# A cross-attention and mixture-of-experts kernel: two experts take 256 tokens each before the routing is complete

## The chip, the cores and the metric

The kernel runs on one core of a Trainium2 chip, in 32-bit floating point. A time is the device time of one execution in microseconds; where a median is given, it is over three executions. The profile is of one more execution, recorded with every instruction and every DMA.

The engines are TensorE (PE, with its weight loads as PEld), VectorE (DVE), ScalarE (ACT), GpSimd (POOL) and SyncE (SP, which here only issues DMAs and loads registers). Each takes its own instructions in the order of the built program, and waits on semaphores for the others. SP, ACT and POOL issue DMAs into queues of their own.

## What is computed

`x` is 8 batches of 256 tokens, 512 wide. Attention over a second input comes first (32 heads of 16, 8 groups), then 32 experts of which each token takes four. Every pair of experts shares a smaller one.

```python
x = x + xattn(layernorm(x), ctx, ctx)            # Wq, Wk, Wv, softmax, Wfc, bfc
h = layernorm(x)
logits = h @ gate_w.T                            # 32 experts
w, sel = top4(softmax(logits)); w = w / w.sum()
large = sum over e of w_e * (silu(h @ Wg[e]) * (h @ Wu[e])) @ Wd[e]            # 192 wide
small = sum over e of w_e * (silu(h @ cWg[e//2]) * (h @ cWu[e//2])) @ cWd[e//2]  # 128 wide
out = x + large + 0.05 * small
```

There are 2048 x 4 = 8192 pairs of token and expert. How many each expert gets depends on the data.

## The kernel before

**Stage 1, attention.** One loop runs over the slots: 16 for each batch, in which the score products of one part, the softmax of the part ten slots earlier (`LAG`) and one or two other steps of other batches (`slots`, L553) are issued in an order that is written out by hand. The wrappers `pe`, `dve` and `act` (class `InOrder`, L39) keep that order for TensorE, VectorE and ScalarE. The steps of a tile of 128 tokens after its attention are those of `finish`: `turn` (transpose), `fc0` and `fc1` (output projection, then the normalised `row`, which goes to the DRAM tensor `xn_all`), `turn_h`, `route` (L472: logits, the best four, their weights) and `place` (L511: for each of its four choices a place in that expert's list, and on POOL one indirect DMA for each choice that scatters token number and weight into the DRAM tensor `lists`, L536). `lists` has room for 2048 entries for each expert; its first 512 entries were filled with numbers of empty rows (`NO_ONE`), which stand behind the tokens in `xn_all` and `out`.

The loop routes the tiles up to number 13. The last two, 14 and 15, are finished behind the loop (L647 to 655), one step after another, with `dve` and `act` no longer held to the written order.

**Ranking, L659 to 682.** TensorE sums `taken` (the choices of all tokens) to `count`; a few VectorE operations compare all counts with one another to `rank` and `at_rank`; one more product gives `order`, the experts by size.

**Stage 2, the experts.** The experts run one after another (L961). The program is built with fixed shares: `CAPS` (L28) lists how many pairs the largest, the second largest and so on may have; `RANKS` puts the two smallest first. For the n-th expert SP loads its number into a register (`expert`), then fetches its list (`list_of`, L707) and its weights (`weights_of`, L694: `wm` 1280 KB and `sm` 768 KB, in four buffers). POOL gathers its rows, one indirect DMA for each 128 (`tokens_of`, L717, line 720). TensorE transposes them (`turned`, `ept` at L744), and does five products of 128 columns of weights by the share's tokens (`inner`, L754: `pu_g`, `pu_u`, `pu_ug`, `pu_gs`, `pu_us`, L764). `down` (L796) does the second products `py`: for two full tiles together at L851, 854 and 856, for a remainder of up to 64 at L839 to 843. `evict` (L804) scales them by the pair's weight and stores them with an indirect DMA on POOL that adds to `out` (L820). The stores of one expert wait for those of the expert before (L977 to 985), since they may add to the same rows. The transposes of the next expert lie between the products of this one.

An expert with more pairs than its share leaves tiles over: `beyond` (L861) works out which, and a loop at the end (L991) handles them, one tile of 128 at a time, as many times as a register says.

SP's issues at the start of stage 2 come in the order that the code has them, from L954 on:

```python
for i in range(3):
    fetch_list(i)
fetch_weights(0)
fetch_tokens(0)
fetch_weights(1)
fetch_tokens(1)
fetch_weights(2)
fetch_list(3)
```

Of the kernel before, what the change touches and what calls it, by code (L numbers as in the profile page):

```python
# [10 lines left out]
F32 = mybir.dt.float32  # L11
I32 = mybir.dt.int32
U32 = mybir.dt.uint32
AF = mybir.ActivationFunctionType
ALU = mybir.AluOpType
# [10 lines left out]


CAPS = [400, 352, 336] + [320] * 3 + [304] * 4 + [288] * 4 + [272] * 5  # L28
CAPS += [256] * 2 + [240] * 6 + [224] * 3 + [208, 192]

# [32 lines left out]
def xattn_moe(ctx: ExitStack, tc, x, ctxT, wqT, wkT, wvT, wfcT, bfc, gateT, wx, ws, out):  # L63
# [35 lines left out]
    def counting(name, n, step, per_partition, base=0):  # L99
# [7 lines left out]
    token_i, _ = counting("token", NT, P, 1)  # L107
# [13 lines left out]
    nc.vector.memset(nothing, 0.0)  # L121

# [3 lines left out]
        no_one[:, :, 0].bitcast(I32), [[1, NO_ONE]], base=B * S, channel_multiplier=0  # L126
# [15 lines left out]
    with ExitStack() as att:  # L142
        aw = att.enter_context(tc.tile_pool(name="aw", bufs=1))
        a2 = att.enter_context(tc.tile_pool(name="a2", bufs=2))
        a3 = att.enter_context(tc.tile_pool(name="a3", bufs=3))
        a6 = att.enter_context(tc.tile_pool(name="a6", bufs=6))
# [43 lines left out]
        def load_ctx(b):  # L190
            t = a3.tile([P, KC, S], F32, tag="ctx", name=f"ctx_{b}")
            nc.scalar.dma_start(out=t, in_=kmajor(ctxT)[:, :, b * S : (b + 1) * S])
            return t

        wq_sb = aw.tile([P, KC, E], F32, tag="wq", name="wq_sb")
        wk_sb = aw.tile([P, KC, P], F32, tag="wk", name="wk_sb")
        wv_sb = aw.tile([P, KC, P], F32, tag="wv", name="wv_sb")
# [22 lines left out]
        def norm(t):  # L220

            xns[t] = a2.tile([P, E], F32, tag=f"xn{t % 2}", name=f"xn_{t}")
            of = statistics(acc[t], f"a{t}")

            def scale():
                scaled(xns[t], acc[t], of)
                nc.gpsimd.tensor_tensor(acc[t], acc[t], bfc_sb, ALU.add)

            later.append(scale)

        def project(b):
# [6 lines left out]
            xT = a2.tile([P, KC, S], F32, tag="xT", name=f"xT_{b}")  # L238
            qT = [a3.tile([P, KC, S], F32, tag=f"qT{r}", name=f"qT_{b}_{r}") for r in range(2)]
            kT = a2.tile([P, 2, S], F32, tag="kT", name=f"kT_{b}")  # L240
            k1 = a3.tile([P, 2, S], F32, tag="k1", name=f"k1_{b}")
# [179 lines left out]
        def finish(t):  # L421
# [12 lines left out]
            def fc(h):  # L434
                half = slice(h * (E // 2), (h + 1) * (E // 2))
                pm = ps_m.tile([P, E // 2], F32, tag="pm", name=f"pmf_{t}_{h}")
                for kc in range(KC):
                    pe.matmul(
                        pm,
                        lhsT=box["oT"][:, kc, :],  # L440
                        rhs=wfc_sb[:, kc, half],
                        start=(kc == 0),
                        stop=(kc == KC - 1),
                    )
                dve.tensor_tensor(acc[t][:, half], pm, acc[t][:, half], ALU.add)
                if h == 0:
                    return
                row = box["row"] = a3.tile([P, E], F32, tag="row", name=f"row_{t}")

                def stats():  # L450
                    of = statistics(acc[t], f"f{t}")
                    act.dma_start(out=out[t * P : (t + 1) * P, :], in_=acc[t])

                    def scale():
                        scaled(row, acc[t], of)
                        later.append(
                            lambda: act.dma_start(out=xn_all[t * P : (t + 1) * P, :], in_=row)
                        )

                    later.append(scale)  # L460

                later.append(stats)
# [84 lines left out]


# [37 lines left out]

        slots_of = {s: what for s, what in enumerate(first)}
# [33 lines left out]
        for s in range(16 * B + LAG + 6):  # L621
# [12 lines left out]
            if s == len(first):  # L634
# [5 lines left out]
                    out=xn_all[B * S :, :].rearrange("(j p) r -> p j r", p=P),  # L640
                    in_=nothing.unsqueeze(1).to_broadcast([P, NS, E]),
                ))
            if slot == 4 and b + 2 < B:
                load_x(b + 2)
                ctxs[b + 2] = load_ctx(b + 2)

        dve, act = nc.vector, nc.scalar  # L647
        last = [finish(t) for t in (NT - 2, NT - 1)]
        for i, name in (
            (0, "turn"), (1, "turn"), (0, "fc0"), (0, "fc1"), (1, "fc0"), (1, "fc1"),  # L650
            (0, "turn_h"), (0, "route"), (1, "turn_h"), (0, "place"), (1, "route"), (1, "place"),
        ):
            last[i][name]()
            while later:
                put_off()

        pm = ps_m.tile([NE, 1], F32, tag="pm", name="pm_count")  # L659
        pe.matmul(pm, lhsT=taken, rhs=ones[:, :1], start=True, stop=True)  # L660
        pr = ps_m.tile([NE, NE], F32, tag="pm", name="pm_counts")
        pe.matmul(pr, lhsT=ones[:, :NE], rhs=taken, start=True, stop=True)
        count = const.tile([NE, 1], F32, tag="count", name="count")
        nc.vector.tensor_copy(count, pm)
        key = const.tile([NE, 1], F32, tag="key", name="key")
        nc.vector.scalar_tensor_tensor(
            key, count, float(NE), part_f[:NE], ALU.mult, ALU.subtract
        )
        more = const.tile([NE, NE], F32, tag="more", name="more")
        nc.vector.scalar_tensor_tensor(  # L670
            more, pr, float(NE), iota_e[:NE], ALU.mult, ALU.subtract
        )
        nc.vector.tensor_scalar(more, more, key, None, ALU.is_gt)
        rank = const.tile([NE, 1], F32, tag="rank", name="rank")
        nc.vector.tensor_reduce(rank, more, AX.X, ALU.add)
        at_rank = const.tile([NE, NE], F32, tag="at_rank", name="at_rank")
        nc.vector.tensor_scalar(at_rank, iota_e[:NE], rank, None, ALU.is_equal)

        pm = ps_m.tile([1, NE], F32, tag="pm", name="pm_order")
        pe.matmul(pm, lhsT=part_f[:NE], rhs=at_rank, start=True, stop=True)  # L680
        order = const.tile([1, NE], I32, tag="order", name="order")
        nc.vector.tensor_copy(order, pm)


    wts = ctx.enter_context(tc.tile_pool(name="wts", bufs=4))
    m1 = ctx.enter_context(tc.tile_pool(name="m1", bufs=1))
    m2 = ctx.enter_context(tc.tile_pool(name="m2", bufs=2))
    m3 = ctx.enter_context(tc.tile_pool(name="m3", bufs=3))
    m6 = ctx.enter_context(tc.tile_pool(name="m6", bufs=6))
    ps_x = ctx.enter_context(tc.tile_pool(name="ps_x", bufs=2, space=bass.MemoryType.PSUM))  # L690
    ps_u = ctx.enter_context(tc.tile_pool(name="ps_u", bufs=3, space=bass.MemoryType.PSUM))
    ps_y = ctx.enter_context(tc.tile_pool(name="ps_y", bufs=3, space=bass.MemoryType.PSUM))

    def weights_of(e_r, n, after=None):  # L694
# [9 lines left out]
        nc.sync.dma_start(out=sm, in_=ws[bass.ds(e_r, 1), :, :].rearrange("o p n -> (o p) n"))  # L704
# [32 lines left out]
    def turned(n, rows, ns):  # L737
# [3 lines left out]
        def chunk(kc):  # L741
            pt = ps_x.tile([P, NS * P], F32, tag="pt", name=f"ept_{n}_{kc}")
            for j in range(ns):
                nc.tensor.transpose(  # L744
# [9 lines left out]
    def inner(n, xT, wm, sm, acts, w, between=lambda kc: None):  # L754
# [6 lines left out]
        def product(cols, name):  # L761
            pu = ps_u.tile([P, NS * P], F32, tag="pu", name=f"pu_{n}_{name}")
            for kc in range(KC):
                nc.tensor.matmul(  # L764
# [96 lines left out]
    def beyond():  # L861
# [8 lines left out]
        nc.vector.tensor_copy(has[:, 1:2], count)  # L870
        nc.vector.tensor_reduce(has[:, 2:3], ps, AX.X, ALU.add)
        over = m1.tile([NE, 1], F32, tag="over", name="over")
        nc.vector.tensor_tensor(over, count, has[:, 2:3], ALU.subtract)
# [32 lines left out]
        done = m1.tile([P, 1], F32, tag="done", name="done")  # L906
        nc.vector.tensor_tensor(done, lo[:, 0:1], lo[:, 1:2], ALU.subtract)
# [6 lines left out]
        nc.sync.dma_start(out=tbl_f, in_=done)  # L914
# [8 lines left out]
    def expert(i):  # L923
        if ("expert", i) not in held:
# [3 lines left out]
        return held["expert", i]  # L928

    def fetch_list(i):  # L930
        if i < NE:
            entries = lists.rearrange("(e n) c -> e n c", e=NE)[
                bass.ds(expert(i), 1), : ns_of[i] * P, :
            ]
            held["list", i] = list_of(
                entries.rearrange("o n c -> (o n) c"), i, ns_of[i],
# [3 lines left out]
    def fetch_weights(i):  # L940
        if i < NE:
            held["weights", i] = weights_of(expert(i), i, gathers.get(i - 1) if i < 3 else None)
# [4 lines left out]


    for i in range(3):
        fetch_list(i)  # L950
    fetch_weights(0)
    fetch_tokens(0)
    fetch_weights(1)
    fetch_tokens(1)  # L954
    fetch_weights(2)
    fetch_list(3)
    now = turned(0, held["tokens", 0], ns_of[0])
    for kc in range(KC):
        now[1](kc)
    before = []  # L960
    for i in range(NE):  # L961
        fetch_tokens(i + 2)
        fetch_weights(i + 3)
        fetch_list(i + 4)
        wm, sm = held["weights", i]
        acts = units[i % 2]
        if i + 1 < NE:
            then = turned(i + 1, held["tokens", i + 1], ns_of[i + 1])
            inner(i, now[0], wm, sm, acts, SHARES[i], then[1])
        else:  # L970
            inner(i, now[0], wm, sm, acts, SHARES[i])
        now = then
        li = held["list", i]
        stores = down(i, acts, wm, sm, li, lambda j: li[:, j, 1:2], SHARES[i])
# [11 lines left out]
        before = stores  # L986
# [88 lines left out]
```

## Time and profile before

| | us |
|---|---|
| median of three executions (lowest, highest) | 1044.01 (1042.89, 1044.69) |
| the profiled execution | 1044.12 |
| its span, first to last instruction | 1042.2 |

| engine | busy us of the span | instructions |
|---|---|---|
| PE | 973.0 (93%) | 4960 |
| PEld | 583.9 (56%) | 4960 |
| DVE | 410.4 (39%) | 918 |
| POOL | 320.7 (31%) | 333 |
| ACT | 317.1 (30%) | 553 |

The mean granted TensorE clock is 0.975 of full. DMA moves 129.39 MB in all.

How to read what follows. The page has rows of 40 digits: the span in 40 slices of 26 us, each digit the busy share in tenths (9 is 90% or more); in the row PEclk it is the clock that TensorE was granted, in tenths of full speed. A line of the timeline gives start, length, engine and line of the code, the operation with its output and input, the count, and in brackets how long the engine was idle before it and what ended that. In the chain of waits, which is followed back from the last instruction, each piece is start, length and what it was. PE instructions are counted as two records for a 32-bit product: a product over four blocks of 128 rows shows as x8. Stage 1 ends at about 462 us of the span, and the first product of stage 2 starts at 504.9.

### The profile page before, as it was taken

Reading aid. Unit: us, or ns where it says so; the run is one execution under the profiler, and the core shown is the slowest. Engines: PE = TensorE matmul, PEld = TensorE weight load, DVE = VectorE, ACT = ScalarE, POOL = GpSimd, SP = SyncE. Lnnn points to the kernel's source line nnn. Section 1 sums busy time; section 2 is a strip of 40 time slices with the busy share of each in tenths; the row PEclk is TensorE's granted clock in tenths of the full one; section 3 lists DMA queues with packets and bytes.
Section 4 is the critical chain, followed back from the end, with each engine's and each line's share of the span. In section 5 each row is a group of like instructions: output and inputs, shape, how many; then the busy total and the mean of one; then the engine's idle time right before and its main releaser. Section 6 shows DMA issues by size and latency. Waiting matters only on the chain.

```text
span 1042.2 us, 13463 instructions
## 1 busy us (share of the span) xinstructions
PE 973.0 (93%) x4960; PEld 583.9 (56%) x4960; DVE 410.4 (39%) x918; ACT 317.1 (30%) x553; POOL 320.7 (31%) x333
## 2 busy tenths in 40 slices
PE   6989999999999997993799999999999999999994
PEld 4534555555555653452565565656666666777772
DVE  4555666666676657433122122212222222122220
ACT  2245544545454544440211121111121212111110
POOL 4100131313121203033352524444343434433221
PEclk9999999999999999996799999999999999999998
DMA  6301010101010000001986775767676767777622
GB/s 214 107 2 42 31 52 32 52 32 33 31 32 21 23 12 32 11 32 43 401 294 134 212 201 168 227 172 207 181 218 187 212 176 209 232 220 224 183 37 36
DMA packets 56197, 129.39 MB, mean 124 GB/s; under 512 B 20545, under 2 KB 25922, under 8 KB 52034
## 3 DMA queue, kind: packets, MB, share of 16 engines
q1 hardware_dynamic: 26802, 75.21, 20.1%
q0 software_dynamic: 18912, 40.12, 18.3%
q10 hardware_dynamic: 10416, 13.18, 3.5%
q8 instruction: 40, 0.66, 0.3%
q14 instruction: 27, 0.22, 0.1%
HBM read 100.56 MB, written 27.66 MB: 123 GB/s over the span
## 4 chain that ended last, share of the span: by engine, by line
PE 50%; issue 1%; DMA 1%; POOL 1%; DVE 0%; POOLq 0%; ACT 0%
PE pu_g L764 6%; PE py L856 6%; PE pu_us L764 6%; PE pu_gs L764 6%; PE pu_ug L764 6%; PE pu_u L764 6%; PE py L851 5%; PE ept L744 4%; PE py L854 3%; PE py L839 2%; PE py L843 1%; DMA rows<-xn_all,li 1%; POOL lists L536 0%; POOL out_dram L820 0%; DVE exT L750 0%
## 5 line engine op out<-in xcount | busy, mean ns | idle before, releaser
L49 DVE TENSOR_REDUCE mx<-sc 128x4 f32<-128x1024 f32 x128 | 156.6, 1223 | 92.9 <-PE st L49 69.9
L49 ACT ACTIVATE pT<-st 128x1024 f32<-128x1024 f32 x128 | 131.0, 1024 | 143.5 <-PE st L49 137.3
L49 PE MATMUL sc<-kT,qT 32*128 32x512 f32 x512 | 145.4, 644 | 17.4 <-DVE mx L49 16.2
L820 POOL DMA_INDIRECT out_dram<-y,li x84 | 128.5, 1529 | 93.3 <-ACT y L818 75.0
L720 POOL DMA_INDIRECT rows<-xn_all,li x84 | 82.3, 980 | 237.2 <-DMA li<-lists 98.3
L49 PE MATMUL st<-qT,k 32*128 32x512 f32 x512 | 146.4, 648 | 0.5 <-DMA qT<-mT 0.5
L536 POOL DMA_INDIRECT lists<-ent,slot_i x64 | 62.4, 975 | 107.8 <-DVE slot_i L49 87.4
L750 DVE COPY exT<-ept 128x384 f32<-128x384 f32 (+2 forms) x64 | 32.5, 508 | 115.6 <-PE ept L744 114.7
L818 ACT ACTIVATE y<-py,li 128x512 f32<-128x512 f32 (+2 forms) x35 | 24.0, 687 | 174.4 <-PE py L856 161.8
L744 PE MATMUL ept<-ident,rows 128*128 128x128 f32 x336 | 59.0, 279 | 19.1 <-DMA rows<-xn_all,li 18.7
L816 DVE TENSOR_SCALAR y<-py,li 128x512 f32<-128x512 f32 (+3 forms) x31 | 23.3, 750 | 129.5 <-PE py L856 129.5
L49 PEld LDWEIGHTS sc<-kT,qT 32*128 32x128 f32 x512 | 38.5, 184 | 58.0 <-DVE mx L49 33.4
L764 PE MATMUL pu_g<-exT,wm 128*128 128x240 f32 (+11 forms) x256 | 67.1, 406 | 0.0
L49 PE MATMUL pmq<-xT,wq_sb 128*128 128x256 f32 x264 | 65.5, 392 | 1.0 <-ACT xT L49 1.0
L744 PEld LDWEIGHTS ept<-ident,rows 128*128 128x128 f32 x336 | 45.0, 143 | 37.2 <-DMA rows<-xn_all,li 19.3
L856 PE MATMUL py<-sm,b 128*128 128x512 f32 x132 | 65.6, 617 | 0.0
L764 PE MATMUL pu_gs<-exT,sm 128*128 128x240 f32 (+11 forms) x256 | 64.6, 395 | 0.0
L764 PE MATMUL pu_us<-exT,sm 128*128 128x240 f32 (+11 forms) x256 | 64.6, 395 | 0.0
L764 PE MATMUL pu_u<-exT,wm 128*128 128x240 f32 (+11 forms) x256 | 64.6, 395 | 0.0
L764 PE MATMUL pu_ug<-exT,wm 128*128 128x240 f32 (+11 forms) x256 | 64.6, 395 | 0.0
L49 PEld LDWEIGHTS pmq<-xT,wq_sb 128*128 128x128 f32 x264 | 47.5, 189 | 30.1 <-issue 22.0
L49 PE MATMUL po<-pT,va 128*32 128x512 f32 x512 | 64.2, 619 | 0.1
(187 smaller groups left out, 1275.4 us busy)
## 6 DMA issues: line engine op xcount, KB each, us to landing
wm<-in_wx_dram SPq DMA_DIRECT2D x32, 1280.0 KB
sm<-in_ws_dram SPq DMA_DIRECT2D x32, 768.0 KB
acc<-in_x_dram SPq DMA_DIRECT2D x16, 256.0 KB
ctx<-in_ctxT_dram ACTq DMA_DIRECT2D x8, 512.0 KB
out_dram<-acc ACTq DMA_DIRECT2D x16, 256.0 KB
xn_all<-row ACTq DMA_DIRECT2D x16, 256.0 KB
rows<-xn_all,li POOLq DMA_INDIRECT x84
out_dram<-y,li POOLq DMA_INDIRECT x84
```

The lines of the kernel that those rows point to most:

```text
L49: this = instruction(*args, **kwargs)
L536: nc.gpsimd.indirect_dma_start(out=list_views[TOPK * t + k], out_offset=bass.IndirectOffsetOnAxis(ap=slot_i[:, k : k + 1], axis=0), in_=en ...
L720: gathers[n] = nc.gpsimd.indirect_dma_start(out=rows[:, j, :], out_offset=None, in_=xn_all, in_offset=bass.IndirectOffsetOnAxis(ap=li[:, j ...
L744: nc.tensor.transpose(pt[:, j * P : (j + 1) * P], rows[:, j, kc * P : (kc + 1) * P], ident)
L750: nc.vector.tensor_copy(xT[:, kc, : ns * P], pt[:, : ns * P])
L764: nc.tensor.matmul(pu[:, :w], lhsT=cols(kc), rhs=xT[:, kc, :w], start=(kc == 0), stop=(kc == KC - 1),)
L816: nc.vector.tensor_scalar(y[:m], py[j][:m], weight(j)[:m], None, ALU.mult)
L818: nc.scalar.activation(y[:m], py[j][:m], AF.Copy, scale=weight(j)[:m])
L820: nc.gpsimd.indirect_dma_start(out=out, out_offset=bass.IndirectOffsetOnAxis(ap=li[:m, j, 0:1].bitcast(I32), axis=0), in_=y[:m], in_offset ...
L851: nc.tensor.matmul(py[i], lhsT=a[:, s], rhs=wa, start=True, stop=False)
L854: nc.tensor.matmul(py[i], lhsT=at[half, s], rhs=wt[half], start=False, stop=False)
L856: nc.tensor.matmul(py[i], lhsT=b[:, s], rhs=wb, start=False, stop=True)
```

## The change

Two experts do part of their tokens early. When six of the eight batches are routed, a ranking of the counts so far chooses the two largest experts. Each does its first 256 entries (or fewer, if it has fewer) while the last tiles are finished.

- In batch 7, at slots 9, 10, 12 and 14 of the loop, four new functions run: `count_ahead` (the ranking, and `done`, the number of entries that an expert does early), `choose_ahead` (the numbers of the two), `fetch_ahead` (two register loads, two lists and eight DMAs of weights on SP) and `gather_ahead` (four gathers on POOL). Rows and weights land in buffers of attention that are no longer needed: `xn`, `xT`, `k1`, `ctx` and the weights `wq`, `wk`, `wv`. The pools are opened in another order for it.
- Behind the loop the steps of `ahead(n)` stand between those of the last two tiles, on TensorE in the written order: four transposes of two tiles, the five products 256 columns wide, the second products. The results `y` stay in memory and are stored when the gathers of the first two experts of stage 2 are issued.
- `dve` and `act` stay held to the written order to the end of this part, and TensorE to the end of the first expert of stage 2.
- The last ranking is by what is left (`took` is subtracted). A second row, `begin`, gives each expert's first entry that is not done. SP loads two registers for each expert, eight of them before anything else, and the weights of the first expert before the lists.
- The shares 400 and 336 leave `CAPS`, 160 and 128 come in: 8800 becomes 8352, and 84 tiles become 80. The two smallest, which run first, are now 128 and 160.
- The empty rows stand ahead of the tokens in `xn_all` and `out`; 256 entries more of each list are filled with their numbers.
- The pools of stage 2 are opened with `reuse_waits="tile"`: a tile that lies on memory of a closed pool waits for those who used that memory.

```diff
-CAPS = [400, 352, 336] + [320] * 3 + [304] * 4 + [288] * 4 + [272] * 5
-CAPS += [256] * 2 + [240] * 6 + [224] * 3 + [208, 192]
+AHEAD, AHEAD_OF = 2, B - 2
+CAPS = [352] + [320] * 3 + [304] * 4 + [288] * 4 + [272] * 5 + [256] * 2 + [240] * 6
+CAPS += [224] * 3 + [208, 192, 160, 128]
...
+        def count_ahead():
+            count, rank, at_rank = ranked("so_far")
+            done = const.tile([NE, 1], F32, tag="done", name="done_ahead")
+            dve.tensor_scalar(done, rank, float(AHEAD), None, ALU.is_lt)
+            dve.scalar_tensor_tensor(done, count, float(S), done, ALU.min, ALU.mult)
+            took = const.tile([NE, NE], F32, tag="took", name="took")
+            dve.tensor_scalar(took, ident[:NE, :NE], done, -1.0, ALU.mult, ALU.mult)
...
+        def gather_ahead():
+            for n in range(AHEAD):
+                rows = [b2.tile([P, E], F32, tag=f"xn{j}", name=f"ahead{n}_{j}") for j in range(2)]
+                for j in range(2):
+                    nc.gpsimd.indirect_dma_start(
+                        out=rows[j],
...
+        do_ahead = {9: count_ahead, 10: choose_ahead, 12: fetch_ahead, 14: gather_ahead}
...
+        for step in early[0]["turn"]:
+            step()
+        for i, name in ((0, "turn"), (1, "turn"), (0, "fc0"), (0, "fc1"), (1, "fc0"), (1, "fc1")):
+            end(i, name)
+        end(0, "turn_h")
+        early[0]["g"]()
+        end(0, "route")
+        end(1, "turn_h")
+        early[0]["u"]()
+        end(0, "place")
+        end(1, "route")
+        early[0]["ug"]()
+        end(1, "place")
+        count, _, at_rank = ranked("count", first_ones["took"])
+        early[0]["gs"]()
...
+        early[0]["gated"]()
+        early[0]["gated_tail"]()
+        early[0]["us"]()
+        early[0]["gated_small"]()
+        for step in early[1]["turn"]:
+            step()
+        early[1]["g"]()
+        early[1]["u"]()
+        early[1]["gated"]()
+        early[0]["second"]()
+        early[1]["ug"]()
+        early[1]["gated_tail"]()
+        early[1]["gs"]()
+        early[1]["us"]()
+        early[1]["gated_small"]()
+        early[1]["second"]()
...
+    for i in range(4):
+        numbers(i)
+    fetch_weights(0)
     for i in range(3):
         fetch_list(i)
-    fetch_weights(0)
     fetch_tokens(0)
     fetch_weights(1)
     fetch_tokens(1)
     fetch_weights(2)
     fetch_list(3)
+    with tc.issue_after(gathers[1].ins):
+        for n in range(AHEAD):
+            in_turn([
+                nc.gpsimd.indirect_dma_start(
+                    out=out,
...
+                    in_=y,
+                    in_offset=None,
+                    compute_op=ALU.add,
+                )
+                for j, y in enumerate(first_ones["y", n])
+            ])
```

## The prediction

> **What bounds the kernel now.** I read the busy rows of the page first, then the busy time by stretch around the end of the attention part, then the chain of waits.
>
> ```profile
> PE   6989999999999997993799999999999999999994
> PEclk9999999999999999996799999999999999999998
> 464.00:505.00 41.00, 17.01 (x83) 13.88 (x84) 12.97 (x59) 3.13 (x10) 17.04 (x19) 0.64 0.34 121
> 505.00:1026.00 521.00, 521.00 (x2150) 336.31 (x2150) 115.79 (x271) 99.62 (x212) 200.19 (x158) 1.00 0.70 198
> ```
>
> The second pair comes from the view by stretch: length, busy us of PE, PEld, DVE, ACT and POOL with their instructions, granted clock, DMA share, GB/s. From 505 on TensorE is busy 521 of 521 us at full clock: a matmul taken out there shortens the kernel by its own time. Between 464 and 505 it is busy 17 of 41: a hole. What makes it, from the timeline of POOL and TensorE and from the chain:
>
> ```profile
> 478.94 1.04 POOL L536 DMA_INDIRECT lists<-ent,slot_i  x1 [5.41 <-issue]
> 487.88 0.96 POOL L536 DMA_INDIRECT lists<-ent,slot_i  x1 [0.30 <-issue]
> 493.22 0.98 POOL L720 DMA_INDIRECT rows<-xn_all,li  x1 [4.39 <-issue]
> 498.17 0.69 PE L744 MATMUL ept<-ident,rows 128*128 128x128 f32 x2 [15.76 <-DMA rows<-xn_all,li]
> 501.79 0.69 PE L744 MATMUL ept<-ident,rows 128*128 128x128 f32 x2 [2.94 <-DMA rows<-xn_all,li]
> 505.11 1.92 PE pu_g L764 x8
> ```
>
> Route of the last tile, eight scatters on POOL, the list back on SP, two gathers, transposes: a latency chain ending in the first product.
>
> **Part 1, stage 2 loses work.** Shares 400 and 336 go, 160 and 128 come. The chain of waits has the products:
>
> ```profile
> 516.84 1.60 PE pu_g L764 x8
> 530.51 2.69 PE pu_g L764 x8
> 545.27 1.72 PE py L851 x4
> 546.98 1.06 PE py L854 x4
> 548.04 1.91 PE py L856 x4
> 549.96 0.86 PE py L851 x2
> 553.54 0.58 PE py L843 x4
> 575.65 2.26 PE pu_g L764 x8
> ```
>
> The product at 530.51 is of the share of 400, that at 575.65 of 336. 2.69/(8 x 400) = 0.84 ns per column and record. Removed: five products each, 5 x 2.69 + 5 x 2.26 = 24.8; second products 8.85 (545.27 to 553.54 + 0.58) and 7.27 (588.27 to 595.54 in the chain); 28 transposes of 0.11 (three take 0.33 at 577.91), 3.1. Together 44.0. Added: products of 160 and 128 columns, 8 x 160 x 0.84 ns = 1.08 and 0.86, five each, 9.7 (0.5 more if a weight load, 0.14 by its group's mean, binds at 128 columns); second products 2.57 for a full tile (549.96 to 552.53) twice and 1.59 for the 32 left over; 12 transposes, 1.3. Together 17.8 to 18.3: -26.1 to -25.6, of which I take **-25.7**. Nothing hides it: the second stretch is full.
>
> It holds only if no pair falls outside the shares. Counting the reference's inputs, the two largest experts have 314 and 248 pairs after six batches; 256 and 248 go early, 141 and 88 remain, under 160 and 128, and each other count stays within its share (329 in 352, 220 in 224). The loop of extra passes runs zero times, as now.
>
> **Part 2, the early work on TensorE.** Per expert: 8 transposes 0.9, five 256-column products 5 x 1.73 (the pu_u row at 879.64) = 8.65, second products 1.72 + 1.06 + 1.91 = 4.69: 14.2, two experts 28.4. The hole offers 24 us idle, and part of the early work is placed behind the routing, so I lay out the order, with last-tile durations of the trace:
>
> - 462.3 to 481.9: turn 0, the attention output projection (7.2), row transposes, routing and placing of both tiles, with g, u and ug of expert 0 between them; before, the count came at about 480.5.
> - 481.9 to 486.7: gs, order and begin, us, turns of expert 1. Then a gap of about 2.1: g of expert 1 needs copies which on VectorE stand behind the ranking, and on ScalarE behind the first silus.
> - 488.8 to 507.0: g, u, second of 0, ug, gs, us, second of 1, without waits by the trace's durations (18.2).
> - Then the first share's transposes and their copies, 1.7. First product of stage 2 at about **508.8** (0.35 for clock included) against 504.9: **+3.9**.
>
> The clock is the first place where a rule weighs:
>
> ```profile
> 475.00:477.00 2.00, 1.48 (x7) 1.49 (x8) 1.45 (x8) 0.51 (x1) 0.00 (x0) 0.63 0.33 127
> 477.00:479.00 2.00, 1.29 (x7) 1.15 (x6) 1.14 (x10) 0.17 (x1) 0.06 (x1) 0.50 0.00 0
> 506.00:508.00 2.00, 2.00 (x13) 2.00 (x12) 0.00 (x0) 1.15 (x2) 0.00 (x0) 0.94 1.01 414
> ```
>
> The granted clock (third from the right) fell at 476, after stretches 62 to 74% busy, and came back after 506. The Trainium skill ("TensorE: Matmul & The Clock Gate", Part 1) puts the drop at an idle window of about 3.4 us; by that a 2.1 gap costs nothing. By the row, a half-busy stretch can drop it: each such window doubles at most 3.4 us of work, +1.7. I take 0.35 at this place, between 0 and 3.4 (two windows). Before, the first product of stage 2 ran at half clock (1.92 against 1.3 for pu_u behind it): -0.6 after.
>
> **Part 3, lists, rows and queues.** Scatters start some 0.9 later and end near 490. Order and begin are ready at 485; SP then makes eight register loads (0.8 each by the six at 482.7 to 487.5) where it made three before the first list, and the weights of the first expert (2.05 MB) now go ahead of the lists. By the skill, "DMA: Bandwidth & Descriptors", Queues, rings and completion order, descriptors of one issuing engine are consumed in ring order on each of the same 16 DMA engines: against this change, since the list then stands behind 2 MB, 5 us at the 400 GB/s of the stretch from 500. But the list waits anyway: its tile lies on weights of early expert 1, so it may not land before the product ug, about 498.3. Then list 500.5, gather 501.4. By the same page's fit (Anatomy of one DMA: 2.0 us plus bytes over 436 GB/s) 256 KB land 2.6 us later, at 504.5; by the rows of the first fence they took 4.0 (494.2 to 498.17) and 6.3 (495.5 to 501.8), the second beside the weights. The weights come earlier now, so I take 3.5: 505, behind TensorE's 507.0, waiting 0 by either row but the last (+0.7).
>
> The POOL queue is in order. Behind gather 1 stand the four early stores, those of expert 1 waiting for those of expert 0 to land (about 5 us in the full DMA stretch: issued 516.25 to 517.9, done near 522.8), and the gathers of experts 2 and 3 behind stores that wait likewise. Rows 2 are needed at 518, and land 515 to 519; rows 3 at 530, and land 529 to 533. I take **+1.3**, ends 0 and 6.
>
> **Part 4, what batch 7 gets.** Count and order, 0.7 on TensorE, eleven small VectorE operations (2 us, beside TensorE work, VectorE being idle at 416 to 420), 4.2 MB of weights and four gathers near 422 to 433, where DMA is at most 2% busy, needed at 462, so 25 us of cover. On SP the loads stand, behind a wait for the early order, before the copies of `mT` into `qT` (four at 438.7 to 440.4), by when they are issued. If that cover went, turn 0, first in TensorE's order, would hold up everything. Against it stands that TensorE's clock there falls to .50 once (416 to 420), which 0.7 more work may avoid: between -2 and +1.5, I take 0 of it beyond the 0.7, which the start at 462.3 contains. The longer fills of lists and zero rows lie under the first batches.
>
> The end: the last expert has 192 pairs where it had 224: its stores begin 0.3 sooner, -0.3.
>
> **Sum** against the profiled run's own span: 1042.2 - 25.7 + 3.9 - 0.6 + 1.3 - 0.3 = 1020.8; that run took 1044.1, 1.9 around the span, and the median is 1044.0: **1022.5**.
>
> **Rivals.**
>
> *The POOL chain takes over (12%).* Stores that each wait 5 us for a landing, ahead of gathers 2 and 3. For it: the POOL rows above, and a 400 GB/s start of the stage. Against it: the trace's waits by DMA in stage 2 are near zero with the same rule of order. Price: two landings not covered, +5 to +12 instead of 1.3: 1027 to 1033.
>
> *Lists or clock (6%).* The routing chain grows, or the half-clock stretch covers much of the 18 us behind 488: +5 to +9 of 18, 1028 to 1032. For it, the 476 row; against it, work that is nearly continuous.
>
> *Slower: extra passes (5%).* If the shares don't hold what is left (the overflow loop's count, read at the end), each pass runs alone: two register loads 1.6, list 1.9, weights and gather side by side 7, transposes 1.2, products 4.8, second products 2.6, evict and store 3.5: about 22 us. From the first on the gain is gone to within 2 us, from the second on it is slower: 1066. For it, the sum of shares falls from 8800 to 8352 for 8192 pairs; against it, the count above.
>
> *The choice does not come in time, or work is doubled (1%)*: rows landing after 486 instead of 433; same time or slower.
>
> **Chances and range.** Forecast 76%, its own range 1017 to 1027 (clock 0 to 3.4, POOL 0 to 4, attention -2 to +1.5); the first two rivals reach 1033; I also keep 1015 for no stall, no gap and the gain of clock in batch 7. Range **1015 to 1032**. A difference under 0.2% (2 us) can't be told from none: faster 0.93, same 0.015, slower 0.055.
>
> **What would show it.** Products of 1.08 and 0.86 first in stage 2, no 2.69 row; stage 2 still full with about 495 us of TensorE; first pu_g at 507 to 511, ending after second products of the early experts, not on a wait for rows; no idle before transposes of experts 1 to 3 above 2 us; granted clock above .5 from 489 on. Wrong, if any extra pass runs, if TensorE waits for rows or lists over 5 us between 487 and 535, or if the attention part ends over 2 us later than 462.

## The result, and the profile after

| | before | changed |
|---|---|---|
| median of five executions, us (lowest, highest) | 1044.01 (1042.89, 1044.69) | 1036.57 (1033.40, 1038.18) |
| ratio, 95% interval | | 0.9924 (0.9902 to 0.9945) |
| profiled execution, its span | 1044.12, 1042.2 | 1037.31, 1035.4 |

Faster, but by 7.4 us of the 21.5 that were forecast, and above the range of 1015 to 1032. The rows that answer to those of before, first from the page (busy tenths in slices of 26 us, granted clock, DMA), then by stretch:

```profile
PE   6979999999999998999859999999999999999994
PEclk9999999999999999999989999999999999999997
DMA  6201110101010000502894767676767677777722
464.00:505.00 41.00, 38.33 (x184) 28.43 (x182) 17.63 (x73) 7.60 (x18) 14.11 (x15) 1.00 0.35 104
505.00:1021.00 516.00, 501.32 (x2120) 328.92 (x2120) 112.08 (x266) 95.88 (x210) 200.61 (x159) 0.99 0.71 200
```

The old hole is filled: between 464 and 505 TensorE is busy 38.3 us of 41 at full clock (17.0 of 41 before). But a new one has opened behind it, where TensorE was never idle: in stage 2 it is busy 501.3 of 516 us. The timeline of TensorE shows where, at the transposes of experts 1, 2 and 3 of stage 2 (start, length, and in brackets the idle time before and what ended it):

```profile
508.26 0.33 PE L51 MATMUL ept<-ident,rows 128*128 128x128 f32 x1 [1.78 <-DMA rows<-xn_all,li]
518.71 0.30 PE L979 MATMUL ept<-ident,rows 128*128 128x128 f32 x1 [2.23 <-DMA rows<-xn_all,li]
520.54 0.37 PE L979 MATMUL ept<-ident,rows 128*128 128x128 f32 x1 [1.53 <-DMA rows<-xn_all,li]
...
539.98 0.44 PE L979 MATMUL ept<-ident,rows 128*128 128x128 f32 x1 [4.86 <-DMA rows<-xn_all,li]
542.47 0.47 PE L979 MATMUL ept<-ident,rows 128*128 128x128 f32 x1 [2.05 <-DMA rows<-xn_all,li]
544.24 0.47 PE L979 MATMUL ept<-ident,rows 128*128 128x128 f32 x1 [1.30 <-DMA rows<-xn_all,li]
544.51 4.26 PE L999 MATMUL pu_u<-exT,wm 128*128 128x352 f32 x8
```

The waits of TensorE for rows from 505 on come to 12.5 + 1.8 = 14.3 us in the waits view. The transposes of one expert's rows lie between the products of the expert ahead of it; so below, "the wait at expert n" is the one for rows of expert n + 1: 1.8 us at expert 0, 4.3 at expert 1, 8.2 at expert 2. The last row of the fence is their follow-up: pu_u of the share of 352 takes 4.26 us where the next product of the same width takes 2.53; the granted clock had fallen to 0.50 meanwhile (538 to 548 in the view by stretch). Why the rows are late, from POOL's timeline:

```profile
501.11 0.95 POOL L955 DMA_INDIRECT rows<-xn_all,li  x1 [0.30 <-issue]
502.36 1.63 POOL L1221 DMA_INDIRECT out_dram<-y_ahead,li_ahead  x1 [0.30 <-issue]
504.30 1.58 POOL L1221 DMA_INDIRECT out_dram<-y_ahead,li_ahead  x1 [0.30 <-issue]
506.18 1.01 POOL L955 DMA_INDIRECT rows<-xn_all,li  x1 [0.30 <-issue]
...
517.43 1.62 POOL L1221 DMA_INDIRECT out_dram<-y_ahead,li_ahead  x1 [7.70 <-ACT sg L1007]
519.35 1.58 POOL L1221 DMA_INDIRECT out_dram<-y_ahead,li_ahead  x1 [0.30 <-issue]
530.16 1.57 POOL L1055 DMA_INDIRECT out_dram<-y,li  x1 [9.22 <-DMA out_dram<-y_ahead,li_ahead]
532.03 1.01 POOL L955 DMA_INDIRECT rows<-xn_all,li  x1 [0.30 <-issue]
```

Read it from the top. The stores of early expert 0 go out at 502.4 and 504.3, ahead of the gathers of expert 2. The stores of early expert 1 come next, and wait for the first two to land: the row at 517.43 names a ScalarE instruction that was done earlier; what ended the wait was the landing (in lists_free below, with the same order, the row names it). The first store of stage 2 waits again, 9.2 us, for the second pair. Only then, at 532, the gathers of expert 3 are issued, for rows that the transposes needed at 535.

To compare kernels I cut each profile at the third record of `pmn` (a transpose early in stage 1), the first product of stage 2, and the end of TensorE's work:

| profiled execution, us | to `pmn` | to the first pu_g | stage 2 | tail |
|---|---|---|---|---|
| before | 67.1 | 437.8 | 521.8 | 15.5 |
| changed | 64.2 | 441.0 | 515.4 | 14.8 |
| stores_late | 63.9 | 440.9 | 499.8 | 14.5 |
| one_late | 66.1 | 440.9 | 506.2 | 14.6 |
| hold_weights | 67.4 | 440.7 | 507.3 | 14.8 |
| small_pieces | 66.0 | 440.9 | 507.6 | 14.6 |
| big_first | 66.0 | 441.3 | 511.6 | 14.8 |
| lists_free | 64.0 | 440.6 | 515.7 | 14.7 |
| lists_first | 63.9 | 440.9 | 497.4 | 14.8 |
| late_small | 63.7 | 440.6 | 498.1 | 14.7 |
| together | 66.4 | 440.5 | 496.8 | 14.7 |

The first column varies by 3.7 us among the changed kernel and its edits, none of which touches that part (see the end); the third is the one to read. Each row is one profile.

### The profile page after: what moved, and what is told of

It is laid out like the page before. It is cut to its first block, busy times and chain, and to the rows that moved or that the text cites. A ratio compares the mean times of both kernels' runs of the same rounds, so it can differ in the third digit from the quotient of the medians.

```text
span 1035.4 us, 13798 instructions
## 1 busy us (share of the span) xinstructions
PE 974.8 (94%) x5052; PEld 593.1 (57%) x5052; DVE 412.2 (40%) x940; ACT 319.0 (31%) x563; POOL 321.3 (31%) x333
## 5 line engine op out<-in xcount | busy, mean ns | idle before, releaser
L1055 POOL DMA_INDIRECT out_dram<-y,li x80 | 122.5, 1532 | 82.6 <-ACT y L1053 53.5
L1053 ACT ACTIVATE y<-py,li 128x512 f32<-128x512 f32 (+1 forms) x33 | 22.7, 687 | 163.8 <-PE py L1091 153.4
L979 PE MATMUL ept<-ident,rows 128*128 128x128 f32 x308 | 54.9, 276 | 12.5 <-DMA rows<-xn_all,li 12.5
L999 PE MATMUL pu_u<-exT,wm 128*128 128x240 f32 (+10 forms) x248 | 63.4, 401 | 0.0
L51 PE MATMUL pmf<-wfc_sb,oT 128*128 128x256 f32 x256 | 63.0, 391 | 0.2 <-ACT oT L51 0.2
L999 PE MATMUL pu_g<-exT,wm 128*128 128x240 f32 (+10 forms) x248 | 62.6, 395 | 0.0
L51 PEld LDWEIGHTS pmf<-wfc_sb,oT 128*128 128x128 f32 x256 | 46.2, 189 | 26.8 <-issue 15.2
L1091 PE MATMUL py<-sm,b 128*128 128x512 f32 x124 | 61.6, 617 | 0.0
L999 PE MATMUL pu_gs<-exT,sm 128*128 128x240 f32 (+10 forms) x248 | 60.6, 387 | 0.0
L999 PE MATMUL pu_us<-exT,sm 128*128 128x240 f32 (+10 forms) x248 | 60.6, 387 | 0.0
```

Source lines behind the costliest of these rows:

```text
L51: this = instruction(*args, **kwargs)
L979: tensor.transpose(pt[:, j * P : (j + 1) * P], rows[:, j, kc * P : (kc + 1) * P], ident)
L999: tensor.matmul(pu[:, :w], lhsT=cols(kc), rhs=xT[:, kc, :w], start=(kc == 0), stop=(kc == KC - 1),)
L1053: nc.scalar.activation(y[:m], py[j][:m], AF.Copy, scale=weight(j)[:m])
L1055: nc.gpsimd.indirect_dma_start(out=out, out_offset=bass.IndirectOffsetOnAxis(ap=li[:m, j, 0:1].bitcast(I32), axis=0), in_=y[:m], in_offset ...
L1091: nc.tensor.matmul(py[i], lhsT=b[:, s], rhs=wb, start=False, stop=True)
```

## The experiments

All start from the changed kernel. Each ratio is to the kernel before, executed beside it (7 to 17 executions, medians 1044.0 to 1044.15); a median is of four executions where no other count is given. The theories: **Q**, the POOL queue, where gathers stand behind stores that wait for landings; **D**, the full DMA engines; **L**, lists that come late; later **P**, the size of the packets beside which rows travel, and **R**, the ring ahead of the lists.

**stores_late**

```diff
-    with tc.issue_after(gathers[1].ins):
-        for n in range(AHEAD):
-            in_turn([...])            # the early stores
...
         in_turn(stores)
+        if i == 8:
+            for n in range(AHEAD):
+                in_turn([...])
```

> The four early stores move from behind the second gather of stage 2 to behind the stores of the ninth expert. Theory Q (the POOL queue is the cause: the gathers of experts 2 and 3 stand behind stores that wait for landings of 10 us): the waits of TensorE for rows between 505 and 545 us (14.3 us in the changed kernel, and some 4 us of half clock with them) fall under 4 us, about 1019 to 1024 us. Theory D (the 16 DMA engines are full, and rows come late whatever stands before them): at most 5 us are gained, 1031 to 1036 us.

1021.47 us (1020.90 to 1024.50), ratio 0.9791 (0.9770 to 0.9812). Stage 2 loses 15.6 us by moving four stores, with as many bytes moved in all. POOL's timeline, the same place:

```profile
505.54 0.94 POOL L955 DMA_INDIRECT rows<-xn_all,li  x1 [0.30 <-issue]
516.10 1.62 POOL L1055 DMA_INDIRECT out_dram<-y,li  x1 [9.62 <-ACT y L1053]
519.30 0.98 POOL L955 DMA_INDIRECT rows<-xn_all,li  x1 [1.58 <-PE pu_ug L999]
```

The gathers of expert 3 start at 519.3 instead of 532.0, and TensorE comes to their rows at 528.8. POOL's long wait is now one for a result, not for a landing. TensorE's waits for rows are 3.1 us. D alone allowed 5 us: Q holds. But the edit takes the stores' traffic away together with their place in the queue, and the landings tell the two apart (view by line, counted from the start of the issue). Rows of expert 3 take 7.0 and 7.5 us (two of the three gathers; the third is not given) where they took 7.8 to 9.6: there nearly all of the gain is in the order. Rows of expert 2 are issued 3.2 us earlier, and take 7.5 and 7.9 us (likewise) where they took 12.4 to 13.0: there more of it is in the landing.

**one_late** (only the second pair of early stores moves)

```diff
     with tc.issue_after(gathers[1].ins):
-        for n in range(AHEAD):
+        for n in range(1):
```

> Only the two stores of early expert 1 move behind the stores of the ninth expert; those of early expert 0 stay behind the second gather. Theory Q as a chain of two landings (the second pair waits for the first to land, the first store of stage 2 for the second, and the gathers of expert 3 stand behind it): one landing is over before TensorE needs rows 3, so 8 to 11 us of the 15 come back, 1025 to 1029 us, and the wait at expert 2 (4.9, 2.1 and 1.3 us) is gone or under 2; the waits at expert 1 stay (4.3 us), since the gathers of expert 2 still stand behind the first pair. If the count of stores on POOL or in the DMA engines matters and not the chain, about half comes back, 1028 to 1031 us, shared by both places.

1028.62 us (1026.81 to 1039.17; one execution lies above 1030), ratio 0.9878 (0.9816 to 0.9941). The time fits both ranges; the places decide. The wait at expert 2 is gone and that at expert 1 kept (2.5, 1.5 and 0.7 us), as the chain says: of the 15.6 us of stage 2, 9.2 hang on the second pair, 6.4 on the first, which stands ahead of the gathers of expert 2.

**hold_weights** (weights 3 and 4 wait for rows 2 and 3)

```diff
-gathers.get(i - 1) if i < 3 else None
+gathers.get(i - 1) if i < 5 else None
```

> The weights of experts 3 and 4 wait for the rows of experts 2 and 3, as those of 1 and 2 already wait for the rows of 0 and 1; the stores stay. Theory D: rows and stores land in 3 to 5 us where they took 7 and 10, 8 us or more are gained, under 1029 us. Theory Q: the chain of stores and gathers keeps its order and is shorter only by what the landings are quicker, 0 to 5 us gained, 1031 to 1037 us; the next weights could then come late and cost it again.

1032.50 us (1031.11 to 1034.76), ratio 0.9891 (0.9870 to 0.9913). The median lies in Q's range, but its profile has one of the late first columns; stage 2 itself loses 8.1 us, more than Q alone allowed, though the early stores still took 10.3 us to land (median). What went is the wait at expert 2 (8.2 to 0.5 us). The gathers of expert 3 start at the same place, 26.3 us behind the first product of stage 2 (26.8 in the changed kernel), but land in 3.6 to 4.3 us instead of 7.8 to 9.6, since hardly any weights travel beside them (0.01 MB moved on SP's queue from 534 to 542 us, where 1.88 MB moved in the changed kernel). So the load of the DMA engines is part of the price, on top of the order.

**big_first** (208 and 192 first, 160 and 128 last)

> The shares 208 and 192 run first in place of 128 and 160, which run last. The two first experts give TensorE about 8.5 us more work while the queues fill, so by Q and by D alike up to 8 us less waiting, and the last expert is shorter: 1027 to 1031 us. If waits are set by when TensorE frees buffers (no theory so far), nothing is gained: 1036 us.

1035.69 us (1033.56 to 1035.73), ratio 0.9911 (0.9893 to 0.9929): 0.9 us less than the changed kernel in the median, 3.8 in stage 2. The edit is in `RANKS` alone. The two first experts gave TensorE only some 5 us more work, not 8.5 (busy 25.4 us up to the first product of expert 2, for 21.2 in the changed kernel, of which 1.1 is half clock), and the wait at expert 1 shrank (4.3 to 1.4 us). But the chain moved along with them: the second pair was issued at 520.9 (517.4), the last gather of expert 3 at 540.2 (534.6), and the wait at expert 2 stayed (8.1 for 8.2). That the first experts are short is little of what costs.

**lists_free** (list tiles of the first three experts in memory of their own)

```diff
-        li = m6.tile([P, NS + 1, 2], F32, tag="li", name=f"li_{n}")
+        if n in (0, 1, 2):
+            li = ys.tile([P, NS + 1, 2], F32, tag=f"li{n}", name=f"li_{n}")
+        else:
+            li = m6.tile([P, NS + 1, 2], F32, tag="li", name=f"li_{n}")
```

> The list tiles of the first three experts lie in memory that the early experts do not use, so the first list is no longer held until TensorE has done the ug product of early expert 1 (494.9 us in the changed kernel; the last scatter is issued at 486.0). Lists and rows 0 and 1 come some 4 us earlier. Theory L (the late lists start the chain too late): the waits at experts 0 and 1 go (6 us) and 5 to 8 us are gained, 1029 to 1032 us. Theory Q: the stores of early expert 1 still wait for its result (504 us) and for 10 us of landing, so rows 3 stay late: 2 to 4 us gained, 1033 to 1035 us.

1037.27 us (1035.52 to 1048.19, 14 executions), ratio 0.9950 (0.9923 to 0.9977): a miss for both theories, nothing gained. The list's issue did move, from 494.92 to 491.59, but not its arrival, from SP's and POOL's timelines:

```profile
487.26 1.36 SPq L939 DMA_DIRECT2D sm<-in_ws_dram  x1
491.59 1.03 SPq L948 DMA_DIRECT2D li<-lists  x2
...
498.03 0.98 POOL L958 DMA_INDIRECT rows<-xn_all,li  x1 [11.61 <-DMA li<-lists]
...
517.19 1.62 POOL L1224 DMA_INDIRECT out_dram<-y_ahead,li_ahead  x1 [8.01 <-DMA out_dram<-y_ahead,li_ahead]
```

The 2 MB ahead of it in SP's queue were still moving until 496 (2.04 MB from 487 to 496), and the lists' packets came right behind them (870 packets with 0.06 MB from 496 to 499). The list had two holds that ended at nearly the same time, so taking out one shows nothing. The last row is the one promised above: here the profile names the landing as what the second pair waits for.

**small_pieces** (every load of weights cut into pieces of 512 columns, order unchanged)

```diff
-        load = nc.sync.dma_start(out=wm, in_=wx[...])
+        load, *_ = pieces(wm, wx, 5)      # five DMAs of 512 columns
...
-        loads.append(nc.sync.dma_start(out=sm, in_=ws[...]))
+        loads.append(pieces(sm, ws, 3)[-1])
```

> Stores and order as in the changed kernel; every load of weights is cut into pieces of 512 columns, so its packets are 2 KB where they were 10 and 6 KB. Theory P (a row of 2 KB waits on each of the 16 DMA engines behind one large packet of weights, turn by turn, and that makes the landings 7 and 10 us): rows land in 4 to 5 us and the early stores in 6 or less, 5 to 9 us are gained, 1028 to 1032 us. If only bytes matter (2 MB of weights ahead or beside), landings stay within 1 us and so does the time, 1035 to 1038 us; more issues on SP could cost up to 3 us.

1032.02 us (1029.25 to 1033.06), ratio 0.9884 (0.9857 to 0.9911). The same bytes in packets of 2 KB instead of 10 and 6 KB: stage 2 loses 7.8 us. Landings from the view by tile (least, median, most; early stores, then rows of 495 to 548 us), the changed kernel first:

```profile
DMA to landing us min/median/max: 9.6/10.2/12.4
DMA to landing us min/median/max: 3.2/7.1/13.0
```

```profile
DMA to landing us min/median/max: 7.6/8.1/8.5
DMA to landing us min/median/max: 3.3/6.0/7.8
```

The medians fall by 2.1 and 1.1, less than P said; the longest by 3.9 and 5.2, and a transpose waits for the longest. The time is at the upper end of what P expected. Fewer bytes beside the rows are not the reason: from 530 to 536 us, where the rows of expert 3 travel, the DMA engines are as full as before (1.05 of their time, 319 GB/s). The Trainium skill ("DMA: Bandwidth & Descriptors", Queues, rings and completion order) says that each DMA engine takes turns between its queues by whole packets; by that, a row of 2 KB waits behind whatever packet of weights is ahead. The run agrees in direction; it does not show the turns themselves, nor that the page's packets are those that the profile counts, nor that this is all of the 10 us, since 8.1 remain.

**lists_first** (stores late, lists free, and the lists issued ahead of the first weights)

```diff
-    fetch_weights(0)
     for i in range(3):
         fetch_list(i)
+    fetch_weights(0)
```

> Early stores late as in stores_late, list tiles free of the early experts as in lists_free, and the three lists issued ahead of the weights of expert 0 as before the change. In lists_free the list was issued at 491.6 us and still came to POOL only at 498, when the 2 MB ahead of it on SP's queue had landed. Theory R (the ring ahead of the list is the second hold): rows 0 and 1 come 3 to 5 us earlier than in stores_late, its waits at expert 0 (0.8 and 1.9 us) go and those at expert 2 too: 2 to 4 us under stores_late, 1017.5 to 1020 us. Rival: the weights of expert 0 come later by as much as the lists take and TensorE waits for them, no gain or 1 to 2 us of loss, 1021 to 1024 us.

1018.17 us (1015.81 to 1029.90), ratio 0.9782 (0.9713 to 0.9850). Stage 2 takes 2.4 us less than in stores_late, and the wait at expert 0 (1.9 us there) is gone, as R says. Waits view of TensorE from 500 to 560 us, stores_late, then lists_first (us in total, times, longest):

```profile
PE ept L51 <- DMA rows<-xn_all,li: 1.9, 1, 1.9
PE ept L979 <- DMA rows<-xn_all,li: 1.2, 1, 1.2
```

```profile
PE ept L51 <- DVE exT L988: 0.8, 1, 0.8
PE ept L982 <- DMA rows<-xn_all,li: 0.7, 2, 0.4
```

What remains is 0.8 us for a copy of the first transposes, which the forecast had in its start, and 0.7 for rows. The wide interval comes from one execution at 1029.90.

**late_small** (stores late and small pieces)

> stores_late with weights in pieces of 512 columns as in small_pieces. Theory P: rows of experts 1 to 3 land 2 to 3 us sooner, but little of them is waited for any more (4 us): 0 to 3 us under stores_late, 1018.5 to 1021.5 us. If only bytes matter: as stores_late, 1020.5 to 1022.5 us.

1018.89 us (1018.76 to 1019.90), ratio 0.9764 (0.9744 to 0.9784): 1.7 us less stage 2 than stores_late.

**together** (lists_first with small pieces)

> Stores late, lists free and ahead of the first weights, weights in pieces of 512 columns: lists_first and late_small in one. Theory: both take out the same waits (TensorE waits 1.6 us for rows from the first product on in lists_first and 2.1 in late_small, 4.0 in stores_late), so together they give 0 to 1.5 us more than one of them: 1016.5 to 1018.5 us, and the start of stage 2 stays at 504 to 507 us. Rival: the pieces take the weights of expert 0 longer to issue behind the lists (eight issues of 0.4 to 0.6 us), and TensorE waits for them at the first product: 1019 to 1022 us.

1018.24 us (1015.78 to 1020.22), ratio 0.9743 (0.9714 to 0.9772), six executions. Both edits take out the same waits, so their gains don't add: stage 2 is 0.6 us shorter than in lists_first. It is the shortest stage 2 of all, and lists_first, late_small and together can't be told apart by their medians. All three beat both kernels: about 25 us under before, 18 under the change.

## Why the prediction was wrong

The terms of its sum beside the two profiles: start +3.9, stage 2 -25.0 (-25.7, -0.6, +1.3), tail -0.3, in all -21.4. Measured: start +3.2, stage 2 -6.4, tail -0.7, and -2.9 in the first 67 us, in all -6.8.

1. **The work taken out of stage 2 was right, to about 1 us.** With the new waits gone stage 2 is 24.4 us shorter than before (lists_first; 0.7 us of waits for rows left) and 25.0 in together, for -26.3 forecast without stalls.
2. **The start was right**, +3.2 for +3.9. TensorE's gap before g of early expert 1 was 1.2 us (2.1 forecast); the clock was granted in full throughout 464 to 505, so the 0.35 charged for it was not needed. That does not decide between the rule on the clock and the half-busy row of before: the only sparse stretch left, 484 to 486 us at 39% busy, was short, and nothing like the six microseconds at 62 to 74% busy, from 471 to 477 in the kernel before, came up.
3. **The attention part** cost 0.1 of the 0.7 charged (the changed kernel leads by 2.75 us at the `pmn` of 406 us, just ahead of the new products at 408 and 417, and by 2.61 at the `pmu` of 459). Those at 408 fell into time in which TensorE waited anyway: its idle time behind them is 1.8 us where it was 2.05. No gain of clock came.
4. **The lists** came to POOL at 498.5, for 501.4 forecast. Both holds that the prediction named were there, TensorE's ug product and the 2 MB on SP's queue; but it took the first for the only one that binds. lists_free shows that the ring holds the lists nearly as long (498.0 for 498.5), and only lists_first, with both holds gone, gained.
5. **The step that failed is the POOL queue: +1.3, "ends 0 and 6".** Taking the early stores off it is worth 15.6 us of stage 2 (stores_late); with lists and packets mended too it is 17.3 (late_small) to 18.6 (together). The mechanism was named, order included, and given 12% as a rival; its terms were too small, the rival's +5 to +12 too. The landing of an early store was taken as 5 us, "done near 522.8" in the trace of before. No view of that trace gives a landing; it shows only that the next store, at 530.8, had nothing to wait for. Measured from the start of the issue it was 9.6 to 12.4 us. Two such landings stand one behind the other ahead of the gathers of expert 3 (502.4 to 517.4, 519.4 to 530.2), so the error counts twice: rows 3 were forecast to land at 529 to 533, and landed from 540 to 544.

   Rows themselves took 7.1 us in the median (up to 13.0); the 4.0 and 6.3 of the trace of before were counted from the end of the issue, and are 4.9 and 7.3 by the same count. And waits that long went with a fall of the clock (0.50 from 522 to 524 and from 538 to 548): pu_u at 4.26 for 2.53, pu_u of the share of 160 at 2.34 for 1.25, 2.8 us that no term held. The prediction's own sign came true: waits for rows of 6.1 us between 487 and 535, where it allowed 5.
6. **What should have warned**: the trace of before had the DMA engines full until 530, with TensorE never waiting, because the gathers of its first three experts were issued by 503, and no gather on POOL had a store ahead of it that waits for a landing: the first store, at 516, waited for its result, the next, at 530.8, for nothing (rows below). That waits by DMA are "near zero with the same rule of order" was read from that stage, where each store had nearly a whole expert (12 us and more) for its landing. The change put four stores, two deep, where there was no expert yet to cover them.

POOL's timeline of before, the last gather of the first three experts, then the first store of each of the first two:

```profile
502.01 0.94 POOL L720 DMA_INDIRECT rows<-xn_all,li  x1 [0.30 <-issue]
516.25 1.63 POOL L820 DMA_INDIRECT out_dram<-y,li  x1 [13.29 <-ACT y L818]
530.77 1.62 POOL L820 DMA_INDIRECT out_dram<-y,li  x1 [0.30 <-issue]
```

So the profiled execution misses its sum by 18.6 us in stage 2, less 0.7 at the start, 0.4 at the tail and 2.9 in the first 67 us. The last is luck as far as the prediction goes: it had no term for it.

## What to carry to other kernels

Early work has results to put away, and on an in-order queue a store that waits for another store's landing blocks every gather behind it: put such stores where nothing urgent follows. A landing is to be priced under the load that it will meet, and a chain of two of them costs two. Where two waits end at the same time, taking out one shows nothing; both have to go before either can be judged.

## What the hardware did that was not expected

An adding store took 10.2 us to land beside loads of weights (median of the four early stores), 8.1 when the same weights came in packets of 2 KB, and 7.4 in stores_late, where they go at 672 to 682 us and the DMA engines are 0.78 busy (670 to 690). It was taken for a fixed latency of about 5.

The start of stage 1, which the change hardly touches and its edits not at all, did not come out the same each time. View by stretch, before, then changed (clock third from the right):

```profile
55.00:60.00 5.00, 2.37 (x20) 0.88 (x16) 3.84 (x6) 2.05 (x2) 1.17 (x2) 0.91 0.00 0
60.00:65.00 5.00, 5.00 (x33) 1.20 (x28) 1.49 (x2) 1.82 (x3) 0.64 (x1) 0.75 0.01 3
```

```profile
55.00:60.00 5.00, 3.48 (x28) 1.14 (x32) 3.93 (x7) 2.06 (x3) 1.82 (x2) 1.00 0.01 3
60.00:65.00 5.00, 3.87 (x30) 1.15 (x22) 2.56 (x5) 2.18 (x3) 0.00 (x0) 1.00 0.00 0
```

In the first the clock falls for some us near 60, after a stretch in which TensorE is half idle in both (from 53 to 58 us it is busy 1.1 us of every 2.45); in the second it does not. That is worth 1.6 us, and the first score product comes 1.2 us earlier besides (18.05 for 19.28). The two vary separately: the clock falls there in five of the nine edited kernels, whose stage 1 is that of the changed one (0.72 to 0.84 from 60 to 65 us), and one of these, hold_weights (67.4), starts late as well, like before. Whether the change itself makes a fall likelier stays open: of the kernel before there is one profile.
